# One edge tile in each eight chunks loaded row by row by SP in a two-layer graph network on Trainium2

## The chip, the core and the metric

The kernel runs on one core of a Trainium2 chip. Five engines work on their own instruction streams and meet through semaphores: TensorE (PE, matrix products and the loading of their stationary operand, PEld), VectorE (DVE), ScalarE (ACT), GpSimd (POOL) and SyncE (SP). SP does no arithmetic here: it only issues DMA transfers. ACT and POOL issue some as well. The metric is the device time of one execution in microseconds (us). The kernel before took 4951.64 us, the median of 7 runs (4927.57 to 4959.24).

## The reference

There are 12500 nodes with 256 features each and 200000 directed edges, given as `src` and `dst` and sorted by `dst`. Layer 0 normalises, applies a graph convolution twice between two dense products, and adds the input back. Layer 1 normalises, computes four attention heads and adds the input back. Cut to what matters:

```python
def _gcn_conv(h, W, b, src, dst, n):            # src, dst with a loop at each node added
    h = h @ W
    norm = dinv[src] * dinv[dst]                # dinv = 1/sqrt(number of edges into a node)
    return segment_sum(h[src] * norm[:, None], dst, n) + b

h = relu(layernorm(x))                          # layer 0
h = h @ W_pre + b_pre
h = relu(_gcn_conv(h, W1, b1, src, dst, n))
h = relu(_gcn_conv(h, W2, b2, src, dst, n))
x = x + h @ W_post + b_post
h = relu(layernorm(x))                          # layer 1
xt = (h @ weight).reshape(n, heads, out_ch)
alpha = softmax(leaky_relu(l(xt)[src] + r(xt)[dst], 0.01), axis=1)
x = x + broadcast(einsum('nh,nhd->nd', alpha[:n], xt[dst[:n]]))
```

The heavy part is `segment_sum(h[src])`: for each of the 200000 edges a row of 256 numbers is fetched by its node number, and the rows with the same destination are added up. It is done twice.

## The kernel before

**Stages.** A preparation of about 125 us counts the edges, normalises the nodes and writes the scaled rows to a table in device memory (`table1`, rows of 260 numbers: 256 features, a sum of scales, padding). The first convolution reads `table1` (its gathers run from 125 to 2353 us of the profiled span) and writes `table2` (rows of 256). The second reads `table2` (2395 to 4706 us) and also does everything per node that follows: the dense product, the residual, the second normalisation and the attention tables. A short mixing stage ends the kernel.

**Tiles.** The edges are cut into 112 chunks of 1792, each of 14 tiles (`J`) of 128 edges; the last chunk is shorter, so that a convolution has 1563 tiles. In `convolve` the loop over tiles does the following for tile `t`:

- POOL gathers the 128 rows that the tile's node numbers name into a slice of `fgot`, one row to a partition (L1128). `fgot` holds one chunk and has four buffers, so POOL can be at most four chunks ahead of PE.
- DVE makes, once per chunk, 0/1 matrices `fhot` that say which destination each edge belongs to (L1056).
- PE multiplies `fhot` and the rows into the accumulator `facc` (L1133, two instructions per tile), which adds up the rows by destination.

**Chunk ends and windows.** Destinations are worked through in 98 windows of 128 nodes. When a chunk is complete, ACT copies the accumulator to `fsums` (L1063). Steps that come later are entered in a list with a due tile and are carried out in the instruction streams when the loop has come to it (`at` and `run`). Eight tiles after the end of the chunk PE turns `fsums`, and with it the rows `self` of the next window, by transposing (L1019). Thirteen tiles after it DVE adds the turned sums to `buf` at an offset that it reads from memory into a register (L1075, L1079). `buf` holds the sums of two windows and a half, feature by feature. If a window is now complete, `shift` starts its finishing steps, takes a new `buf`, copies to it the part that stays (L1095) and the turned `self` rows (L1099), and calls `ready` for the window after.

**What SP does.** `ready` issues the loads of the next window. In the first convolution these are `fins` (L1152) and `self` (L1013). In the second they are `rb` (L1185), `fxb` (L1189) and `self`. `fins` and `rb` have four buffers and `fxb` three. The finishing steps of the second convolution also let SP store the new rows, `kept_x` (L1223), after DVE has written `fx` (L1221). SP carries these out strictly in the order of the program. The stores to `table2` and to the attention tables are issued by ACT.

**Finishing a window.** In the first convolution: a product with the weights, `fpo` (L1162, L1163), and a relu and a store by ACT. In the second: two products `fpz` and `fpo` (L1200, L1216), the residual `fx`, the normalisation, a turn `fpt` (L1242) and the attention products `fpx` (L1255), spread over 28 tiles.

The functions that the diff touches follow.

Of the kernel before, what the change touches and what calls it, by code (L numbers as in the profile page):

```python
# [8 lines left out]
F32 = mybir.dt.float32  # L9
BF16 = mybir.dt.bfloat16  # L10
I32 = mybir.dt.int32
# [6 lines left out]
P = 128  # L18
# [395 lines left out]
def fast_path(  # L414
# [26 lines left out]
    nc = tc.nc  # L441
    N, D = x.shape
    (E,) = src.shape
    H, C = attn_l.shape
    KC = D // P
    J = 14
    CE = J * P
    NCH = -(-E // CE)
# [5 lines left out]
    BW = OFF + P  # L454
# [11 lines left out]
    const = ctx.enter_context(tc.tile_pool(name="fconst", bufs=1))  # L466
# [25 lines left out]
    src_t = const.tile([P, NCH, J], I32, name="fsrc_t")  # L492
# [14 lines left out]

    bb = const.tile([2, D], F32, name="bb")

    with tc.tile_pool(name="fprep", bufs=1) as prep:  # L510


# [28 lines left out]
        def load_edges(e, pad, name):  # L541
            t = rows_p.tile([NCH, CE], I32, name=name)

            if last < CE:
                nc.vector.memset(t[:, last:], pad)

            some = (NCH - 1) // 16 * 16
            for c0, c1 in ((0, some), (some, NCH - 1)):
                nc.sync.dma_start(t[c0:c1, :],
                                  e[c0 * CE:c1 * CE].rearrange("(c e) -> c e", e=CE))  # L550
            nc.sync.dma_start(t[NCH - 1:NCH, :last], e[None, (NCH - 1) * CE:])
            return t
# [14 lines left out]
        def load_x(g, pool):  # L567
            n0, n1 = g * G * P, min((g + 1) * G * P, N)

            xt = pool.tile([P, G, D1], F32, name="fxt", bufs=XB if g < XB else NG - XB)  # L570
            nc.gpsimd.memset(xt[:, :, D:], 0.0)
            k, r = divmod(n1 - n0, P)
            if k < G:
                nc.gpsimd.memset(xt[:, k:, :], 0.0)
            nc.sync.dma_start(xt[:, :k, :D],
                              x[n0:n0 + k * P, :].rearrange("(c p) d -> p c d", p=P))
            if r:
                nc.sync.dma_start(xt[:r, k, :D], x[n0 + k * P:n1, :])
            xs.append(xt)

        XB = 11
        for g in range(XB):
            load_x(g, prep)
            if g == 1:
                src_r = load_edges(src, 0, "fsrc_r")


        zeros = prep.tile([1, 512], BF16, name="zeros")
# [378 lines left out]
    def convolve(ep, table, stride, width, ahead, with_sum, psum, prepare, finish):  # L967
# [28 lines left out]
        def run(now=None):  # L996

            while due:
                d = min(due, key=lambda d: (d["t"], d["n"]))
                if now is not None and d["t"] > now:  # L1000
                    return
                do(d)

        def new_buf():
            buf = work.tile([P, KC, BW], F32, name="buf", bufs=4)
            sbuf = work.tile([1, BW], F32, name="sbuf", bufs=4) if with_sum else None
            return buf, sbuf

# [14 lines left out]
        def new_turned(v):  # L1023
            v["pt"] = psum.tile([P, 2 * KC, P], F32, name="fturn", bufs=1)
            if with_sum:
                v["ps"] = psum.tile([1, 2, P], F32, name="fsum", bufs=1)

        state["buf"] = new_buf()
        for n0 in range(0, BW, P):
            v, n = {}, min(P, BW - n0)  # L1030
# [21 lines left out]
        def hot_of(c):  # L1052

            n = nj[c]
            h = ep.tile([P, J, P], F32, name="fhot", bufs=3)
            nc.vector.tensor_tensor(h[:, :n, :], iota_p[:, None, :].to_broadcast([P, n, P]),  # L1056
                                    to_t[:, c, :n, None].to_broadcast([P, n, P]), ALU.is_equal)
            return h

        def close(c, acc, t):  # L1060
# [24 lines left out]
            def shift(now):  # L1085
                w = state["w"]
                if w == complete[c + 1]:
                    return

                buf, sbuf = state["buf"]  # L1090
                pre, rows = state["next"]
                steps = finish(w, buf, sbuf, pre, state.get("bias"))
                if w + 1 < NT:
                    nxt, nxs = new_buf()
                    nc.vector.tensor_copy(nxt[:, :, :BW - P], buf[:, :, P:])  # L1095
                    if rows is None:
                        nc.vector.memset(nxt[:, :, BW - P:], 0.0)
                    else:
                        nc.vector.tensor_copy(nxt[:, :, BW - P:], v["pt"][:, KC:, :])  # L1099
                    if with_sum:  # L1100
                        nc.vector.tensor_copy(nxs[:, :BW - P], sbuf[:, P:])
                        if rows is None:
                            nc.vector.memset(nxs[:, BW - P:], 0.0)
                        else:
                            nc.vector.tensor_copy(nxs[:, BW - P:], v["ps"][:, 1, :])
                    state["buf"] = nxt, nxs

                then = None
                for i, (o, step, fills) in reversed(list(enumerate(steps))):
                    then = at(now + (i + 1 if near else o), lambda _, step=step: step(), fills, then)  # L1110
                state["w"] += 1
                ready(w + 1)
                if state["w"] < complete[c + 1]:
                    shift(now)
# [2 lines left out]
            at(t + (2 if c + 1 == NCH else 6 if near else 13), add)  # L1117

        tiles = [(c, j) for c in range(NCH) for j in range(nj[c])]
        hots = {0: hot_of(0)}  # L1120
        for t, (c, j) in enumerate(tiles):
            if j == 0:
                acc = psum.tile([P, width], F32, name="facc", bufs=2 if not with_sum else 3)

            if j == 0:
                gots = ep.tile([P, J, stride], F32, name="fgot", bufs=ahead)
            got = gots[:, j, :]
            nc.gpsimd.indirect_dma_start(  # L1128
                out=got, out_offset=None, in_=table[:],
                in_offset=bass.IndirectOffsetOnAxis(ap=src_t[:, c, j:j + 1], axis=0))  # L1130
            if j == 2 and c + 1 < NCH:
                hots[c + 1] = hot_of(c + 1)
            nc.tensor.matmul(acc, hots[c][:, j, :], got[:, :width], start=(j == 0),  # L1133
                             stop=(j == nj[c] - 1))
            if j == nj[c] - 1:
                close(c, acc, t)
            run(t)
# [37 lines left out]
    with tc.tile_pool(name="psum1", bufs=1, space=PSUM) as psum, \  # L1175
            tc.tile_pool(name="edges1", bufs=1) as ep, \
            tc.tile_pool(name="fwork1", bufs=2) as work:
        convolve(ep, table1, D1, D + 1, 4, True, psum, lambda w: prepare1(work, w),
                 lambda w, b, s, pre, _: finish1(work, psum, w, b, s, pre))
# [123 lines left out]
    ap = ctx.enter_context(tc.tile_pool(name="fatt", bufs=2))  # L1303
# [15 lines left out]
    with tc.tile_pool(name="psum2", bufs=1, space=PSUM) as psum, \  # L1319
            tc.tile_pool(name="edges2", bufs=1) as ep, \  # L1320
            tc.tile_pool(name="fwork2", bufs=2) as work:
        for c in range(EARLY):
            turn_hots(ap, c, load_ends(work, c, 1), EARLY)
        none = work.tile([P, LW, H], F32, name="none", bufs=1)
        nc.vector.memset(none, 0.0)
        nc.sync.dma_start(table_e[(NT - LW) * P:, :].rearrange("(w p) h -> p w h", p=P), none)

        from_all = work.tile([P, CE], I32, name="to_all", bufs=1)
        nc.sync.dma_start(from_all, src[:CE].partition_broadcast(P))
        for i in range(LW):  # L1330
            nc.vector.tensor_scalar(hot_l[i], from_all, float((NT - LW + i) * P), lane,
                                    op0=ALU.subtract, op1=ALU.is_equal)
        convolve(ep, table2, D, D, 4, False, psum, lambda w: prepare2(work, w),
                 lambda w, b, s, pre, bias: finish2(work, psum, w, b, pre, bias))

        for c in range(1, AC):
            own_rows(c)
# [111 lines left out]
def kernel(tc, *args):  # L1449
    nc = tc.nc  # L1450
    with tc.tile_pool(name="flag", bufs=1) as flag:
        bad = flag.tile([1, 1], I32, name="bad")
        with ExitStack() as ctx:
            with tc.manual_schedule():
                fast_path(ctx, tc, bad, *args)
        n_bad = nc.values_load(bad[0:1, 0:1], min_val=0, max_val=1 << 20,
                               skip_runtime_bounds_check_because="a count of chunks")
        with tc.If(n_bad > 0):
            with ExitStack() as ctx:
                general_path(ctx, tc, *args)  # L1460
# [27 lines left out]
```

## Time and profile before

| what | value |
|---|---|
| median of 7 runs | 4951.64 us (4927.57 to 4959.24) |
| the profiled execution's own time | 4976.77 us |
| its span, first to last instruction | 4975.0 us |
| mean granted TensorE clock | 0.709 |
| PE busy | 2659.2 us (53%) |
| POOL busy | 3116.0 us (63%) |
| DVE busy | 1206.1 us (24%) |
| ACT busy | 415.1 us (8%) |
| first convolution: first to last gather | 125 to 2353 us |
| second convolution: first to last gather | 2395 to 4706 us |
| mean load of the 16 DMA engines in the convolutions | 39% and 41% |

The profiled execution is 25 us longer than the median of the runs; its span and its own time differ by 1.8 us. Busy time counts work on data; instructions for registers, semaphores and the issuing of DMA transfers are not counted, so SP has no busy time at all and is read from the timeline and the waits. In a group of instructions the columns are line, engine, operation, output and inputs, number, then busy time and mean ns of one, then the idle time of the engine just before them and what ended most of it. "remote" as a releaser is a semaphore event whose origin the profile does not give; "issue" is time in which the engine waited for nothing that the profile shows. In a timeline the columns are start, duration, engine, line, operation, operands, the number of instructions put together, and the idle time before. A wait line names the waiting queue, whom it waited for, and the total, number and longest of the waits.

### The profile page before, as it was taken

The numbers are of one execution on the slowest core, as the hardware profiler recorded it, in microseconds if no ns is written. First come the engines' busy times: TensorE is split into PE (matmuls) and PEld (weight loads), VectorE is DVE, ScalarE is ACT, GpSimd is POOL, SyncE is SP. The second block draws the span as 40 slices with busy tenths as digits, with TensorE's granted clock in tenths as the row PEclk, the third lists the DMA queues.
The fourth block names the chain that finished last, engine by engine and source line by source line (L and its number), as shares of the span: only waits on it lengthen the run. The fifth ranks groups of instructions, "written<-read, shape, count | busy, mean of one in ns | idle before, by whom it ended". The sixth has DMA issues, their size and how long they took to land. (4 is left out here: it accounts for less than half of the span.)

```text
span 4975.0 us, 31762 instructions
## 1 busy us (share of the span) xinstructions
PE 2659.2 (53%) x10363; PEld 2032.3 (41%) x10363; DVE 1206.1 (24%) x2541; ACT 415.1 (8%) x1084; POOL 3116.0 (63%) x3346
## 2 busy tenths in 40 slices
PE   5355655555555655555454555555555455555553
PEld 4244433333444433333343444444444344444441
DVE  7121111111212111112221222222222222222236
ACT  5000000000000000000000100010011000000011
POOL 3666666666666666666566566666665566666533
PEclk6666666666666766666677777777777777777776
DMA  7433333333333333333334333444343344444335
GB/s 228 113 103 104 105 106 105 105 107 102 105 106 104 105 106 106 103 107 97 112 105 110 103 106 108 114 112 113 102 113 104 99 113 108 110 111 108 102 100 159
DMA packets 325909, 551.10 MB, mean 111 GB/s; under 512 B 96009, under 2 KB 224232, under 8 KB 325736
## 3 DMA queue, kind: packets, MB, share of 16 engines
q0 software_dynamic: 153520, 414.27, 31.2%
q1 hardware_dynamic: 126678, 118.54, 7.9%
q10 hardware_dynamic: 45538, 16.17, 1.3%
q8 instruction: 86, 1.41, 0.1%
q14 instruction: 87, 0.71, 0.1%
HBM read 495.47 MB, written 53.19 MB: 110 GB/s over the span
## 5 line engine op out<-in xcount | busy, mean ns | idle before, releaser
L1128 POOL DMA_INDIRECT fgot<-ftable,fsrc_t x3126 | 2974.1, 951 | 1616.6 <-issue 916.9
L1133 PE MATMUL facc<-fgot,fhot 128*128 128x257 f32 (+1 forms) x6252 | 1842.1, 437 | 553.3 <-issue 521.8
L1133 PEld LDWEIGHTS facc<-fgot,fhot 128*128 128x128 f32 x6252 | 1337.1, 222 | 897.1 <-issue 685.7
L1079 DVE TENSOR_TENSOR buf<-buf,fturn 128x256 f32 x224 | 94.5, 422 | 2059.4 <-remote 1633.8
L1056 DVE TENSOR_TENSOR fhot<-iota_p,to_t 128x1792 f32<-128x1792 f32 x224 | 448.3, 2003 | 0.1
L1242 PE MATMUL fpt<-fident,h 128*128 128x128 f32 x194 | 59.9, 407 | 607.9 <-ACT h L1237 538.8
L1162 PE MATMUL fpo<-wf,buf 128*128 128x256 f32 x388 | 149.6, 525 | 394.8 <-DVE buf L1079 298.5
L1242 PEld LDWEIGHTS fpt<-fident,h 128*128 128x128 f32 x194 | 27.1, 188 | 647.9 <-ACT h L1237 571.2
L1162 PEld LDWEIGHTS fpo<-wf,buf 128*128 128x128 f32 x388 | 96.2, 261 | 454.4 <-issue 339.3
L1216 PE MATMUL fpo<-fwo,fz 128*128 128x256 f32 x388 | 126.1, 454 | 255.3 <-issue 94.0
L1207 DVE SCALAR_TENSOR_TENSOR fy<-rb,fb2c,fpz 128x128 f32<-128x128 f32 x194 | 58.7, 344 | 737.5 <-remote 412.0
L1063 ACT ACTIVATE fsums<-facc 128x257 f32<-128x257 f32 (+1 forms) x224 | 85.8, 383 | 1808.4 <-remote 1361.4
L1221 DVE SCALAR_TENSOR_TENSOR fx<-fpo,fdinv,fxb 128x256 f32<-128x256 f32 x97 | 46.9, 483 | 737.2 <-remote 512.5
L1216 PEld LDWEIGHTS fpo<-fwo,fz 128*128 128x128 f32 x388 | 77.0, 218 | 269.9 <-ACT fz L1210 127.7
L1019 PE MATMUL fturn<-fident,fsums 128*128 128x128 f32 x448 | 105.4, 324 | 91.9 <-ACT fsums L1063 71.6
L1255 PE MATMUL fpx<-fwg,ht 128*128 128x4 f32 (+1 forms) x388 | 62.0, 267 | 171.8 <-ACT ht L1246 115.6
L1200 PE MATMUL fpz<-buf,fwb 128*128 128x128 f32 x776 | 152.7, 363 | 0.0
L1200 PEld LDWEIGHTS fpz<-buf,fwb 128*128 128x128 f32 x776 | 145.6, 277 | 1.1 <-DVE fy L1207 0.2
L1255 PEld LDWEIGHTS fpx<-fwg,ht 128*128 128x128 f32 x388 | 64.2, 210 | 185.2 <-ACT ht L1246 120.1
L1019 PEld LDWEIGHTS fturn<-fident,fsums 128*128 128x128 f32 x448 | 76.5, 174 | 140.4 <-ACT fsums L1063 81.3
L1397 POOL DMA_INDIRECT fal<-table_l,fsrc_t x84 | 80.4, 958 | 72.5 <-DVE fs L1404 47.8
L1387 PE MATMUL fends<-rows,hot_t 128*128 128x260 f32 x168 | 68.7, 553 | 96.1 <-issue 60.5
(212 smaller groups left out, 1644.5 us busy)
## 6 DMA issues: line engine op xcount, KB each, us to landing
fgot<-ftable,fsrc_t POOLq DMA_INDIRECT x3126
ftable<-fxt SPq DMA_DIRECT2D x14, 910.0 KB
self<-ftable SPq DMA_DIRECT2D x97, 130.0 KB
ftable<-fo ACTq DMA_DIRECT2D x98, 128.0 KB
kept_x<-fx SPq DMA_DIRECT2D x98, 128.0 KB
self<-ftable SPq DMA_DIRECT2D x97, 128.0 KB
fxb<-in_x_dram SPq DMA_DIRECT2D x97, 128.0 KB
fxt<-in_x_dram SPq DMA_DIRECT2D x13, 896.0 KB
```

Of the source, the lines that this page charges most:

```text
L1019: nc.tensor.transpose(v["pt"][:, i * KC + k, :], rows[:, k * P:(k + 1) * P], ident)
L1056: nc.vector.tensor_tensor(h[:, :n, :], iota_p[:, None, :].to_broadcast([P, n, P]), to_t[:, c, :n, None].to_broadcast([P, n, P]), ALU.is_equal)
L1063: nc.scalar.activation(sb, acc, AF.Copy)
L1079: nc.vector.tensor_add(b, b, v["pt"][:, :KC, :])
L1128: nc.gpsimd.indirect_dma_start(out=got, out_offset=None, in_=table[:], in_offset=bass.IndirectOffsetOnAxis(ap=src_t[:, c, j:j + 1], axis=0))
L1133: nc.tensor.matmul(acc, hots[c][:, j, :], got[:, :width], start=(j == 0), stop=(j == nj[c] - 1))
L1162: nc.tensor.matmul(po, buf[:, k, :P], wf[:, k, :], start=(k == 0), stop=False)
L1200: nc.tensor.matmul(pz[:, m, :], wb[:, k, m * P:(m + 1) * P], buf[:, k, :P], start=(k == 0), stop=(k == KC - 1))
L1216: nc.tensor.matmul(po, v["z"][:, m, :], wo[:, m, :], start=(m == 0), stop=(m == KC - 1))
L1242: nc.tensor.transpose(pt[:, k, :], v["h"][:, k * P:(k + 1) * P], ident)
L1255: nc.tensor.matmul(px, v["ht"][:, k, :], wg[:, k, d0:], start=(k == 0), stop=(k == KC - 1))
L1397: nc.gpsimd.indirect_dma_start(out=al[:, i, :], out_offset=None, in_=(table_l if c else table_e)[:], in_offset=bass.IndirectOffsetOnAxis(a ...
```

## The change

Every eighth chunk, beginning with chunk 3 (3, 11, ..., 99), has its last tile handled in another way: 13 tiles in each convolution. POOL does not gather them. SP reads the tile's 128 node numbers from a small table kept on the chip, `hand_i3`, 32 at a time into registers, and issues one DMA for each row, from the table's row of that number to one partition of a tile `hand3`. So a tile takes four bursts of 32 rows. The bursts are put into SP's stream at fixed places: the first about 132 tiles before the tile is used, the others 28 tiles apart, the last about 48 tiles before. For the first of these tiles there is not so much room, and its four bursts stand at tiles 0, 8, 17 and 26; the first burst of the next follows at 35. PE multiplies from `hand3` in place of `fgot`; the order of PE's, DVE's and ACT's work stays.

`hand3` has two buffers. The table of node numbers, 13 x 128, is loaded once in the preparation by one more DMA on SP. `buf` has three buffers in place of four. In line numbers, the changed kernel's `convolve` is moved down: its gather is at L1163, its matmul at L1168, its `self` load at L1023, its register load at L1145 and its row loads at L1149.

```diff
--- before.py
+++ after.py
@@ -507,6 +507,13 @@
 
     bb = const.tile([2, D], F32, name="bb")
 
+
+    HC = 8
+    HR = 32
+    NH = (E // CE - 1) // HC
+    HANDS = [(eng, of, const.tile([NH, P], I32, name=f"hand_i{of}"))
+             for eng, of in ((nc.sync, 3),)]
+
     with tc.tile_pool(name="fprep", bufs=1) as prep:
 
 
@@ -583,6 +590,9 @@
             load_x(g, prep)
             if g == 1:
                 src_r = load_edges(src, 0, "fsrc_r")
+                for _, of, idx in HANDS:
+                    nc.sync.dma_start(idx, src[:NH * HC * CE].rearrange(
+                        "(i c e) -> i c e", c=HC, e=CE)[:, of, CE - P:])
 
 
         zeros = prep.tile([1, 512], BF16, name="zeros")
@@ -1002,7 +1012,7 @@
                 do(d)
 
         def new_buf():
-            buf = work.tile([P, KC, BW], F32, name="buf", bufs=4)
+            buf = work.tile([P, KC, BW], F32, name="buf", bufs=3)
             sbuf = work.tile([1, BW], F32, name="sbuf", bufs=4) if with_sum else None
             return buf, sbuf
 
@@ -1117,6 +1127,27 @@
             at(t + (2 if c + 1 == NCH else 6 if near else 13), add)
 
         tiles = [(c, j) for c in range(NCH) for j in range(nj[c])]
+
+        hands = {}
+        rows_due = [[] for _ in range(NCH * J)]
+        for eng, of, idx in HANDS:
+            for i in range(NH):
+                due_by = (i * HC + of + 1) * J - 1
+                t0, t1 = max(due_by - HC * J - 20, 0), due_by - 20
+                for e0 in range(0, P, HR):
+                    rows_due[t0 + e0 * (t1 - t0) // P].append((eng, of, idx, i, e0))
+
+        def by_hand(t):
+            for eng, of, idx, i, e0 in rows_due[t]:
+                c = i * HC + of
+                if e0 == 0:
+                    hands[c, J - 1] = ep.tile([P, stride], F32, name=f"hand{of}", bufs=2)
+                _, nodes = nc.values_load_multi_w_load_instructions(
+                    idx[i:i + 1, e0:e0 + HR], engines=(eng.engine,), min_val=0, max_val=N - 1,
+                    skip_runtime_bounds_check_because="a node")
+                for k, n in enumerate(nodes):
+                    eng.dma_start(hands[c, J - 1][e0 + k:e0 + k + 1, :], table[bass.ds(n, 1), :])
+
         hots = {0: hot_of(0)}
         for t, (c, j) in enumerate(tiles):
             if j == 0:
@@ -1124,10 +1155,14 @@
 
             if j == 0:
                 gots = ep.tile([P, J, stride], F32, name="fgot", bufs=ahead)
-            got = gots[:, j, :]
-            nc.gpsimd.indirect_dma_start(
-                out=got, out_offset=None, in_=table[:],
-                in_offset=bass.IndirectOffsetOnAxis(ap=src_t[:, c, j:j + 1], axis=0))
+            by_hand(t)
+            if (c, j) in hands:
+                got = hands.pop((c, j))
+            else:
+                got = gots[:, j, :]
+                nc.gpsimd.indirect_dma_start(
+                    out=got, out_offset=None, in_=table[:],
+                    in_offset=bass.IndirectOffsetOnAxis(ap=src_t[:, c, j:j + 1], axis=0))
             if j == 2 and c + 1 < NCH:
                 hots[c + 1] = hot_of(c + 1)
             nc.tensor.matmul(acc, hots[c][:, j, :], got[:, :width], start=(j == 0),
```

## The prediction

> **What bounds the kernel now.** I read the page's busy times first, then the groups by line, then the timeline of POOL, of PE and of SP in a stretch of a convolution, then SP's waits.
>
> Busy times and costliest groups, from the page:
>
> ```profile
> span 4975.0 us, 31762 instructions
> ...
> PE 2659.2 (53%) x10363; PEld 2032.3 (41%) x10363; DVE 1206.1 (24%) x2541; ACT 415.1 (8%) x1084; POOL 3116.0 (63%) x3346
> ...
> L1128 POOL DMA_INDIRECT fgot<-ftable,fsrc_t x3126 | 2974.1, 951 | 1616.6 <-issue 916.9
> L1133 PE MATMUL facc<-fgot,fhot 128*128 128x257 f32 (+1 forms) x6252 | 1842.1, 437 | 553.3 <-issue 521.8
> ```
>
> No engine is full; POOL is busiest, and 95% of that is the gather of L1128. Its true rate is in the timeline of POOL alone, 1500 to 1530 us, in the first convolution:
>
> ```profile
> 1516.30 0.94 POOL L1128 DMA_INDIRECT fgot<-ftable,fsrc_t  x1 [0.30 <-issue]
> 1517.55 0.95 POOL L1128 DMA_INDIRECT fgot<-ftable,fsrc_t  x1 [0.30 <-issue]
> 1518.80 0.95 POOL L1128 DMA_INDIRECT fgot<-ftable,fsrc_t  x1 [0.30 <-issue]
> 1525.06 0.95 POOL L1128 DMA_INDIRECT fgot<-ftable,fsrc_t  x1 [5.31 <-remote]
> 1526.31 0.94 POOL L1128 DMA_INDIRECT fgot<-ftable,fsrc_t  x1 [0.30 <-issue]
> ```
>
> A gather starts each 1.2526 us, and then POOL stands still for 5.3 us: all four `fgot` buffers are full and PE has not given one back. This repeats each two chunks: 28 x 1.2526 + 5.1 = 40.2 us. In the second convolution the stop is mostly 2 to 3.5 us after each 14 gathers. PE over the same stretch:
>
> ```profile
> 1501.21 1.90 PE L1133 MATMUL facc<-fgot,fhot 128*128 128x257 f32 x8
> ...
> 1514.49 0.59 PE L1133 MATMUL facc<-fgot,fhot 128*128 128x257 f32 x1 [1.51 <-issue]
> 1517.29 0.59 PE L1133 MATMUL facc<-fgot,fhot 128*128 128x257 f32 x1 [2.21 <-issue]
> 1520.09 0.59 PE L1133 MATMUL facc<-fgot,fhot 128*128 128x257 f32 x1 [2.21 <-issue]
> ...
> 1528.10 1.57 PE L1133 MATMUL facc<-fgot,fhot 128*128 128x257 f32 x6
> ```
>
> PE does a burst (two matmuls of a tile in about 0.45 us), then creeps at 2.8 us a tile although the rows are there, and bursts again some us after POOL has stopped. I do not know why it creeps; it goes with POOL issuing. So the two are locked: POOL's gathers and its stop make the period, and one gather fewer should take its 1.25 us out of it.
>
> SP in the second convolution, 3001 to 3043 us (`kept_x` and the three loads of the next window):
>
> ```profile
> 3001.25 0.32 SPq L1223 DMA_DIRECT2D kept_x<-fx  x1
> 3001.62 0.43 SPq L1185 DMA_DIRECT2D rb<-roots  x1
> 3002.10 0.45 SPq L1189 DMA_DIRECT2D fxb<-in_x_dram  x1
> 3002.65 0.38 SPq L1013 DMA_DIRECT2D self<-ftable  x1
> 3021.39 0.32 SPq L1223 DMA_DIRECT2D kept_x<-fx  x1
> ```
>
> and SP's waits over the whole span:
>
> ```profile
> SPq L1223 <- DVE fx L1221: 1304.2, 55, 44.6
> SPq L1152 <- remote: 968.7, 36, 51.0
> SPq L1152 <- PE fpo L1163: 894.7, 48, 98.3
> ```
>
> SP is nearly always waiting. In the first convolution it waits for a free `fins` buffer and so stands three to four windows ahead. In the second it waits for the window's `fx`, works 1.8 us, and is idle for 18.4 us (3003.0 to 3021.4). That idle time is the cover of everything this change gives it.
>
> **The change, part by part.**
>
> *Gathers removed.* 13 per convolution, 26 of 3126. At 1.2526 us: 26 x 1.2526 = 32.6 us, if POOL's gathers set the period throughout. In the second convolution some stops last 8 to 10.7 us and end on PE's `facc`; there a shorter POOL stretch only waits longer. I take nine tenths: 29 us. Ends: 0 (PE sets the period) and 39 us (26 tiles at the second convolution's 1.50 us).
>
> *Rows added.* 26 tiles x 128 = 3328 row loads in 104 bursts on SP: a load of 32 registers, then for each row an address calculation and a DMA. The trace has no DMA with an address from a register and no such load. Nearest rows: SP's DMAs take 0.50 us (`fins`, one row), 0.53 (`self`, first convolution), 0.43 and 0.45 (`rb`, `fxb`), 0.32 (`kept_x`), with 0.05 us between; the address calculation is DVE's FUSED_REGOPS before L1079, 0.07 us; a load of one register is 0.30 us on DVE, 0.77 in SP's only case. Low end for a burst: 32 x (0.32 + 0.05) + 0.3 = 12 us, the calculation hidden. High end: 32 x (0.53 + 0.07 + 0.10) + 32 x 0.30 = 32 us, every register at the price of a load of one. I take 32 x (0.46 + 0.07 + 0.10) = 20 us and 3 us for the registers (between 0.8 and 9.6, nearer to the load that SP has made): 23 us. Over both convolutions 104 x 23 = 2.4 ms of SP's time, of which its 3.2 ms of waits are the cover.
>
> The Trainium skill ("Runtime: NRT & Kernel Launch", section "Instruction fetch mechanics") says a register load costs about 200 ns per register even in bulk; one register at 0.30 us in this trace neither confirms nor denies the bulk price. By that rule the 32 registers would be 6.4 us, the burst 26 us, and the result some 50 us worse than mine.
>
> *What stands behind a burst on SP.* One burst comes each 28 tiles. In the first convolution SP's lead takes it up, but at its start five bursts stand in a row ahead of window 1's `fins` and `self`: 134 + 5 x 23 = 249 us, and PE needs that `self` with tile 63, at 261 us. The second convolution starts likewise: 2416 + 5 x 23 = 2531, needed at 2537. Both just fit at 23 us; at 25 us they are 1 to 12 us late, at 30 us about 52 us together. In the second convolution's steady part, some bursts stand right behind `kept_x` and ahead of `rb`, `fxb` and `self`. There `self`, issued at 3042.9 and landing 2.5 us later, is used by PE's turn (L1019) at 3054.8, so only 9.5 us of the burst are hidden. I laid the new order of SP's stream over the issue times of before, with bursts of one length B, and added how late `self` lands for its turn: B = 18 us: 12 late, 42 us in all; 20: 14, 63; 23: 25, 112; 25: 26, 178; 30: 39, 540. PE's turn blocks the tiles behind it, and those hold POOL's buffers. But a PE that stops while creeping loses 2.8 us for a tile that a burst repairs in 0.45; bursts are about 15 of 40 us. So I let a half reach the end: 56 us at B = 23. Ends: 0 (all repaired) and 112.
>
> *PE's wait for a hand tile.* The rows come over eight DMA lanes, so the matmul has two more semaphore instructions (0.02 us, 52 in all: 1 us). The last burst is placed 48 tiles ahead of the use, some 67 us: hidden unless SP is behind by more than 40 us.
>
> *DMA queues and ACT.* 3328 rows of 1 KB are 3.4 MB beside 551; the DMA engines are at 33 to 40%. ACT's stores share the lanes with the rows: a store may wait for a row's landing, 2 to 5 us, and what it waits for (`fo`, three buffers) has a window's slack. Nothing. If completions of DMAs are what makes PE creep, 3328 more beside 3126 gathers could make it creep longer: unknown, bounded by nothing lost and by one slow tile (2.8 us) for each burst, 104 x 2.8 = 290 us.
>
> The skill's page "DMA: Bandwidth & Descriptors" ("Issuing engines are not separate DMA queues") says that issuing from another engine saves only the issuer's time. That speaks for counting POOL's 1.25 us and no transfer time. The sum is the same by it.
>
> *One more index load in the preparation* (13 x 128 numbers, one SP DMA, 0.5 us, beside `load_x`): under 1 us. *Three `buf` instead of four*: a new `buf` waits for the readers of the one three windows back; those are its own finish, 6 tiles after the shift, while windows are 16 tiles apart. Nothing; if it did wait, DVE's L1095 would show it.
>
> **Sum.** -29 + 56 + 1 + 1 = +29 us, against the profiled 4976.8 us: about 5006. That execution lies 25 us above the median of the runs shown (4951.6), so by the median the forecast is 4980 us, +0.6%. About 0.3% (15 us) is what a measurement of this kernel tells from no change.
>
> **The rivals.**
>
> 1. *Cover holds (faster).* Late `self` loads cost little because PE's backlog of landed tiles repairs them, or B is 18 us or less. Then -29 + 0 to 15: 4923 to 4938 us. For it: PE is 37 tiles behind POOL and has half its time free. Against it: POOL stops for want of buffers in each cycle, so PE has no slack to give. It turns where the stalls that reach the end equal 29 us: B about 20 us with a half, 0.63 us a row all told.
> 2. *No net change.* B is near 20 us, or PE sets the period so that nothing is gained and bursts fit: within 15 us of 4952. The long stops on `facc` speak for it; the first convolution's fixed 40.2 us against it.
> 3. *Long register loads.* B of 28 to 32 us: starts 35 to 70 us late, 300 to 600 us of late loads of which a half counts, less 29: 5080 to 5250 us. Only the one-register price speaks for it. Above 39 us a burst (28 tiles x 1.41 us) SP would set the pace, hundreds of us more; my high end does not reach it.
> 4. *The rows lengthen PE's creeping.* A quarter of the 290 us, less 29: about 4995 us, without any late `self`.
>
> **How the numbers follow.** Forecast (B 21 to 26, 4966 to 5050): 0.32. Rival 1: 0.36 over all its ways, but as a case with one size it is two (a short burst 0.18, a repaired delay 0.18), each less likely than the forecast. Rival 2: 0.14. Rival 3: 0.12. Rival 4: 0.06. Faster 0.36; same 0.14; slower 0.32 + 0.12 + 0.06 = 0.50. The range: down to the full gain with no loss, 4952 - 33 = 4919, taken to 4915; up to the lower part of rival 3, 5110, which leaves out its worse half and little else. The forecast's own range is 4966 to 5050.
>
> **What the profile after would show.** Gathers 3100 in number at the same 1.25 us; SP's bursts by their length (row to row under 0.63 us: rival 1; a register load over 6 us: rival 3); PE's waits on `self` at L1019 up from 21.8 us to about 110 if I am right, unchanged if rival 1 holds; POOL's stops the same length but the chunk pairs with a hand tile 1.25 us shorter; the first 300 us of each convolution without a gap if five bursts fit. I am wrong if SP's time per row is far from 0.63 us, or if PE's late turns vanish in its backlog.

## The result and the profile after

The changed kernel takes 5959 us (median of 19 runs, 5916 to 5997), the kernel before beside it 4954 us (46 runs, 4915 to 4993): a ratio of 1.2035, 95% interval 1.2013 to 1.2058. It is 1005 us slower. One number needs a word ahead of the experiments: the kernel before itself has two speeds, which change between groups of runs and not within one; beside the experiments it took 4958 to 4977 us in four groups and 4234 to 4243 in three, two chips showed both, and each experiment is compared with the kernel before of its own group. Where it takes about 4960 us, PE creeps as the prediction describes; where it takes about 4240 us, nothing creeps. The result was measured where it creeps. (`buf` holds three and a half windows of sums, 448 columns, and not two and a half as the description above has it.)

The busy times and the costliest groups of the changed kernel's page, with the columns as before:

```profile
span 5959.8 us, 41808 instructions
...
PE 2571.3 (43%) x10363; PEld 2022.1 (34%) x10363; DVE 1201.0 (20%) x2541; ACT 415.4 (7%) x1084; POOL 3099.0 (52%) x3320
...
L1163 POOL DMA_INDIRECT fgot<-ftable,fsrc_t x3100 | 2957.2, 954 | 2631.4 <-PE facc L1168 1408.0
L1168 PE MATMUL facc<-fgot,fhot 128*128 128x257 f32 (+1 forms) x6200 | 1784.1, 440 | 236.8 <-issue 228.3
...
L1029 PE MATMUL fturn<-fident,self 128*128 128x128 f32 x396 | 109.9, 372 | 2024.2 <-DMA self<-ftable 1982.1
```

The work costs what it did: a gather 954 ns (951 before), a matmul 440 (437). What is new is idle time. PE stands 1982 us in front of the turn of `self` (21.8 us before), and POOL's idle time has grown from 1617 to 2631 us, more than half of it now ended by PE giving a buffer back. SP, in the same profile, 1521 to 1578 us:

```profile
1529.49 43.66 SPq L1149 DMA_DIRECT2D hand<-ftable  x32
1573.25 0.53 SPq L1187 DMA_DIRECT2D fins<-root_t  x1
1573.83 0.58 SPq L1023 DMA_DIRECT2D self<-ftable  x1
1574.51 0.51 SPq L1187 DMA_DIRECT2D fins<-root_t  x1
1575.07 0.57 SPq L1023 DMA_DIRECT2D self<-ftable  x1
1577.95 1.96 SPq L1149 DMA_DIRECT2D hand<-ftable  x5
```

One burst of 32 rows takes 43.7 us, and two windows' loads wait behind it: SP has fallen behind and gives two `self` together. PE and POOL at the same place:

```profile
1576.24 0.69 PE L1029 MATMUL fturn<-fident,self 128*128 128x128 f32 x2 [35.28 <-DMA self<-ftable]
```

```profile
1522.22 0.94 POOL L1163 DMA_INDIRECT fgot<-ftable,fsrc_t  x1 [4.97 <-remote]
1581.32 0.95 POOL L1163 DMA_INDIRECT fgot<-ftable,fsrc_t  x1 [23.96 <-PE facc L1168]
```

PE waits 35.3 us for the `self` issued at 1573.8, and POOL's stop is 24 us where it was 5. SP's own waits, which were its cover:

```profile
SPq L1258 <- DVE fx L1256: 420.3, 45, 31.6
...
SPq L1187 <- PE fpo L1198: 75.5, 5, 23.6
SPq L1187 <- remote: 71.1, 3, 28.6
```

The waits on `fins` have fallen from 1863 to 147 us, and those on `fx` from 1304 to 420. The 104 bursts, each from its register load to its last row, add up to 4509 us: 46.8 us each in the first convolution, 39.9 in the second. From one hand tile's first burst to the next tile's the median is 202 and 200 us; in the first convolution four bursts of 46.8 are 187 us of that and the seven windows' loads take most of the rest: there SP is the bound. In the second, four bursts are 160 us of the 200, and in the rest SP still waits some 30 us for `fx`, which comes late because PE is late.

How late PE is against the profile of before, tile by tile, shows where the 1005 us came from: 93 us by tile 90, 526 us at the end of the first convolution, 90 us more in the first 112 tiles of the second, 993 us at its end. So the two starts cost 183 us, and the steady part some 40 us for each 112 tiles in the first convolution and some 35 in the second.

Why a burst is long is in the durations of the row instructions (minimum, median, maximum in ns), in this profile:

```profile
L1149 SPq FUSED_REGOPS  x3328: 1/37/1407, 135.9 to 5473.8; - x196
L1149 SPq MOVE hand<-ftable x3328: 1/29/1400, 136.0 to 5473.9; - x196
L1149 SPq DMA_DIRECT2D hand<-ftable x3328: 1/228/1398, 136.0 to 5473.9; - x196
```

and in a profile of the same kernel where nothing creeps (experiment after_again):

```profile
L1149 SPq FUSED_REGOPS  x3328: 37/37/47, 132.6 to 3811.7; - x196
L1149 SPq MOVE hand<-ftable x3328: 29/29/43, 132.6 to 3811.8; - x196
L1149 SPq DMA_DIRECT2D hand<-ftable x3328: 224/228/322, 132.7 to 3811.9; - x196
```

A row is three instructions, 0.41 us from row to row when SP is undisturbed. In the result's profile their records lie in steps of about 0.70 us for long stretches, whatever the instruction: a register operation there lasts 0.70 us, now and then 1.40, instead of 0.04. The length of a single record says little there: 719 of the 3328 DMA instructions are recorded with 20 ns or less, and undisturbed none takes under 224. So the steps are what is read here. Of the steps from row to row, 1587 are under 0.5 us, and 1237 are over 1.2 us and make up 3359 us of the bursts. Sorted by the number of gathers that POOL began in the 12 us before a row, the median step is 0.41 to 0.49 us with none to seven of them, 0.72 with eight, 2.11 with nine and 2.81 with ten. SP creeps like PE, while POOL's gathers follow one another. But the gathers alone do not do it: in after_again nine or ten of them stand in the 12 us before nearly every row, and the median step is 0.41 us.

### The profile page after: what moved, and what is told of

Its sections match the earlier page's. It is cut to its first block, busy times and chain, and to the rows that moved or that the text cites. A ratio compares the mean times of both kernels' runs of the same rounds, so it can differ in the third digit from the quotient of the medians.

```text
span 5959.8 us, 41808 instructions
## 1 busy us (share of the span) xinstructions
PE 2571.3 (43%) x10363; PEld 2022.1 (34%) x10363; DVE 1201.0 (20%) x2541; ACT 415.4 (7%) x1084; POOL 3099.0 (52%) x3320
## 5 line engine op out<-in xcount | busy, mean ns | idle before, releaser
L1163 POOL DMA_INDIRECT fgot<-ftable,fsrc_t x3100 | 2957.2, 954 | 2631.4 <-PE facc L1168 1408.0
L1168 PE MATMUL facc<-fgot,fhot 128*128 128x257 f32 (+1 forms) x6200 | 1784.1, 440 | 236.8 <-issue 228.3
L1168 PEld LDWEIGHTS facc<-fgot,fhot 128*128 128x128 f32 x6200 | 1357.8, 226 | 534.1 <-issue 309.0
L1029 PE MATMUL fturn<-fident,self 128*128 128x128 f32 x396 | 109.9, 372 | 2024.2 <-DMA self<-ftable 1982.1
L1029 PEld LDWEIGHTS fturn<-fident,self 128*128 128x128 f32 x396 | 55.0, 178 | 2060.7 <-DMA self<-ftable 1989.1
L1235 PE MATMUL fpz<-buf,fwb 128*128 128x128 f32 x776 | 137.0, 335 | 0.0
L1202 ACT ACTIVATE fo<-fpo,fdinv 128x256 f32<-128x256 f32 x97 | 46.0, 474 | 1241.7 <-remote 1087.1
L1235 PEld LDWEIGHTS fpz<-buf,fwb 128*128 128x128 f32 x776 | 129.8, 250 | 1.3 <-DVE fy L1242 0.2
L1197 PE MATMUL fpo<-wf,buf 128*128 128x256 f32 x388 | 102.7, 388 | 34.7 <-issue 24.5
L1298 ACT ACTIVATE fxa<-fpx 128x4 f32<-128x4 f32 (+1 forms) x95 | 18.4, 194 | 1299.1 <-PE fpx L1290 720.7
```

Of the source, the lines that this page charges most:

```text
L1029: nc.tensor.transpose(v["pt"][:, i * KC + k, :], rows[:, k * P:(k + 1) * P], ident)
L1163: nc.gpsimd.indirect_dma_start(out=got, out_offset=None, in_=table[:], in_offset=bass.IndirectOffsetOnAxis(ap=src_t[:, c, j:j + 1], axis=0))
L1197: nc.tensor.matmul(po, buf[:, k, :P], wf[:, k, :], start=(k == 0), stop=False)
L1235: nc.tensor.matmul(pz[:, m, :], wb[:, k, m * P:(m + 1) * P], buf[:, k, :P], start=(k == 0), stop=(k == KC - 1))
```

## The experiments

Theory A: SP's time for the rows is the loss; SP cannot finish four bursts and seven windows' loads in the time of 112 tiles, and PE waits for what stands behind the bursts. Theory B: the row transfers and their completions slow PE and POOL themselves. Theory C: the third `buf` is missed.

### The third buffer alone (bufs3)

```diff
-            buf = work.tile([P, KC, BW], F32, name="buf", bufs=4)
+            buf = work.tile([P, KC, BW], F32, name="buf", bufs=3)
```

> The kernel before with three buf instead of four, and nothing else. Theory A (SP is the bound: the row loads take SP longer than the tiles take PE, and the next window's self stands behind them) expects no difference, 4952 us within 15. Theory C (the third buffer of sums makes DVE wait) expects a good part of the 1005 us here.

Measured: 4242 us, the kernel before 4243; ratio 1.000 (0.999 to 1.0009). Theory C falls, for the condition in which this ran; no_rows_2 and fixed_2 below have three `buf` as well and lose nothing where PE creeps.

This run also showed that POOL can go without stops. Its gathers and matmuls:

```profile
L1128 POOL DMA_INDIRECT fgot<-ftable,fsrc_t x3126 | 2973.9, 951 | 975.9 <-issue 901.0
L1133 PE MATMUL facc<-fgot,fhot 128*128 128x257 f32 (+1 forms) x6252 | 2393.7, 501 | 946.9 <-DMA fgot<-ftable,fsrc_t 905.5
```

POOL's idle time is the 0.30 us behind each gather and little else (901 of 976 us), and PE waits for gathered rows. A gather costs the same 951 ns as in the profile of before.

### The gain alone (no_rows, no_rows_2)

```diff
-                    hands[c, J - 1] = ep.tile([P, stride], F32, name=f"hand{of}", bufs=2)
-                _, nodes = nc.values_load_multi_w_load_instructions(
...
-                    eng.dma_start(hands[c, J - 1][e0 + k:e0 + k + 1, :], table[bass.ds(n, 1), :])
+                    hands[c, J - 1] = blank
```

> The changed kernel with no row loads and no register loads: the 26 tiles are neither gathered nor loaded, PE multiplies a tile of zeros for them, so 3328 edges are missing from the sums. This is the gain by itself. If POOL's gathers and its stop set the period: 26 x 1.2526 = 33 us, 4920 us. If PE sets it: 4952 us.

> The kernel of no_rows again (the 26 tiles neither gathered nor loaded, 3328 edges missing), for a chip where PE and SP creep (before near 4960): the gain by itself there. 26 x 1.25 us if the cycle of gathers and stop keeps: 4927 us; 0 if PE sets the period: 4960. Where nothing creeps (before near 4240): 4209, as in no_rows.

Measured where nothing creeps: 4209.6 us against 4243.1, ratio 0.9928 (0.9912 to 0.9945): 33.5 us, close to 26 x 1.2526 = 32.6. Where PE creeps: 4964 against 4971, ratio 0.9974 (0.9952 to 0.9997): 7 us by the medians, 13 by the ratio, 24 at most. So the full gain is there only where POOL alone sets the time. Where PE and POOL are locked, most of a gather saved goes back into waiting: POOL's waits that ended with PE or with a remote event are 670 us in no_rows_2 and 623 in the profile of before.

### Rows loaded and gathers kept (rows_too)

```diff
-            if (c, j) in hands:
-                got = hands.pop((c, j))
-            else:
+            if True:
                 got = gots[:, j, :]
```

> The changed kernel with all 3126 gathers kept on POOL: the rows are loaded by SP as well and nobody reads them. Nothing waits for a hand tile. Theory A expects the same loss as the changed kernel, 5960 to 6000 us, with PE's wait for self near 1980 us. If the matmul's wait for hand tiles were the loss, 4952 us.

Measured: 4251 us against 4243, ratio 1.0018 (1.0007 to 1.0028). Nothing crept in this group, so it does not speak on the 1005 us. It shows that 3328 row loads on SP cost 8 us there, with bursts of 27.5 us (a bare burst is 15.2; the rest is rows waiting for stores of ACT in the DMA lanes: 811 us in 83 waits on the store of `fo` alone).

### One instruction for a row (fixed, fixed_2)

```diff
-                _, nodes = nc.values_load_multi_w_load_instructions(
-                    idx[i:i + 1, e0:e0 + HR], engines=(eng.engine,), min_val=0, max_val=N - 1,
-                    skip_runtime_bounds_check_because="a node")
-                for k, n in enumerate(nodes):
-                    eng.dma_start(hands[c, J - 1][e0 + k:e0 + k + 1, :], table[bass.ds(n, 1), :])
+                for k in range(HR):
+                    n = (1021 * i + 97 * (e0 + k)) % N
+                    eng.dma_start(hands[c, J - 1][e0 + k:e0 + k + 1, :], table[n:n + 1, :])
```

> The changed kernel with fixed row numbers in place of the edges' own: no register loads, and one instruction on SP for each row in place of three (the 26 tiles add up the wrong rows). Theory A with a slow pace per instruction of SP: a row falls from 1.37 us to some 0.6, a burst from 43 us to 18 to 25, SP is no longer the bound: 4950 to 5050 us. Theory B (each row DMA and its completions slow PE and POOL themselves, whoever issues it): 5900 to 5960 us, as the number of DMAs is the same.

> The kernel of fixed again (fixed row numbers, one SP instruction to a row, no register loads). Where PE and SP creep, theory A with a price of 0.70 us for each SP instruction: a row costs 0.70 to 0.9 us in place of 2.1 to 2.8 while POOL gathers, a burst 16 to 25 us, under the 34 at which SP becomes the bound: 4930 to 5010 us. If the price is for each DMA and not for each instruction: 5700 to 5960. Where nothing creeps: 4211, as in fixed.

Measured where nothing creeps: 4211 us, ratio 0.9931 (0.9914 to 0.9948), the same as leaving the rows out. Where PE and SP creep: 4972 against 4971 us, ratio 1.0005 (0.9983 to 1.0026). This is the run that decides between the theories. The 3328 row transfers, their completions, their lanes and the matmuls' waits for them are all there, and the loss is gone but for 7 us against no_rows_2 by the medians, 15 by the ratios, which is about their noise. Theory B falls. What was taken away is two of three instructions per row and the register loads: a burst is 28.2 us in place of 43.4, and PE's waits for `self` are back to small ones:

```profile
PE fturn L1029 <- DMA self<-ftable: 110.9, 26, 13.1
```

The price is one for each instruction: sorted as above, a row's median step here is 0.72 us with nine gathers and 1.38 with ten, 1.4 us less than with three instructions, which is twice 0.70. The burst is a little longer than the expected 16 to 25 us: 648 of its steps from row to row are still over 1.2 us. In part these are waits for ACT's stores in the DMA lanes, the semaphores that the rows share with them (217 us on the store of `fo`, 156 on that of `table_l`).

### The changed kernel again, and the windows' loads on ACT (after_again, on_act)

```diff
-            nc.sync.dma_start(s[:n, :], table[n0:n0 + n, :])
+            nc.scalar.dma_start(s[:n, :], table[n0:n0 + n, :])
```

and in the same way for `fins`, `rb`, `fxb` and `kept_x` (on_act; after_again has no edit).

> The changed kernel itself, beside the kernel before, because the kernel before took 4243 us where the first four experiments ran and 4954 us where the result was measured. If PE and SP again creep while POOL gathers (before at about 4950), theory A expects 5960 us again. If they don't (before at about 4243, POOL's gathers without stops), a row on SP is 0.41 us, POOL alone sets the time, and the change gives its 26 gathers: 4243 - 33 = 4210 us, at most 4225 with some late self loads.

> The changed kernel with the window's loads (fins, self, rb, fxb) and the store of kept_x issued by ACT, so that SP has the row loads alone and nothing stands behind them. Where PE and SP creep: theory A's first half (self behind the bursts) expects most of the loss gone; its second half (SP's capacity: 4 bursts of 43 us in 112 tiles are 172 us against 161 before) leaves the hand tiles themselves late, 5100 to 5400 us; theory B expects 5900. Where nothing creeps: as the changed kernel, 4205 to 4225 us.

Measured, where nothing creeps: 4210.9 us for the changed kernel, ratio 0.9945 (0.9929 to 0.9962), and 4208.1 for on_act, 0.9938 (0.9921 to 0.9954), against 4234. So the same kernel that is 20% slower in the result is 0.55% faster here, by 23 us. Its bursts are 27.2 us. SP in the first convolution:

```profile
1508.01 21.88 SPq L1149 DMA_DIRECT2D hand<-ftable  x32
1529.99 0.52 SPq L1187 DMA_DIRECT2D fins<-root_t  x1
1530.57 0.58 SPq L1023 DMA_DIRECT2D self<-ftable  x1
1531.24 0.52 SPq L1187 DMA_DIRECT2D fins<-root_t  x1
```

The order is the same as in the result's profile, with two windows behind a burst, and the burst half as long. PE waits 661 us for `self` here too (92 waits), and it costs little, because POOL sets the time and PE has time free.

### A longer burst, with the same transfers (pad8, pad16, pad16_act)

```diff
-                for k, n in enumerate(nodes):
+                for k in range(HR):
+                    if k % 4 == 0:                       # pad8; 2 in pad16 and pad16_act
+                        _, nodes = nc.values_load_multi_w_load_instructions(
...
-                    eng.dma_start(hands[c, J - 1][e0 + k:e0 + k + 1, :], table[bass.ds(n, 1), :])
+                    eng.dma_start(hands[c, J - 1][e0 + k:e0 + k + 1, :],
+                                  table[bass.ds(nodes[k], 1), :])
```

pad16_act has the edit of on_act as well.

> The changed kernel with the 32 numbers loaded anew after every 4 rows: 8 register loads of 2.07 us to a burst in place of one, so that SP is longer at a burst by 14.5 us and every transfer stays. Where nothing creeps the bare burst grows from 15.2 to 29.7 us, with waits for the DMA lanes some 36. Theory A (SP's time for four bursts and seven windows against the 139 us that POOL takes for 111 gathers): 4 x 36 + 8 = 152 us for each 112 tiles, 26 x 13 us more than 4211: about 4550 us (4250 to 4600). Theory B (the rows themselves disturb PE and POOL): no change, 4211.

> As pad8, with a new load after every 2 rows: 16 loads to a burst, 31 us more, a bare burst of 46 us, with lane waits 48: the length that it had where PE and SP crept (43 to 47). Theory A: 4 x 48 + 8 = 200 us for each 112 tiles, as in the result's trace (209): 26 x 61 us more than 4211, 5600 to 5900 us, with PE waiting on self. Theory B: 4211.

> pad16 with the windows' loads and stores issued by ACT, so that no self stands behind a burst. If the order on SP is the whole loss: 4210 to 4260 us. If SP's capacity is: hand tiles come late themselves, 4 x 48 = 192 us for each 112 tiles, 5400 to 5700 us, and PE waits at the matmul of the hand tile in place of the turn.

These ran where PE and SP creep (before 4976), and the numbers of theory A are for the other condition: bursts of 52.7, 64.9 and 78.6 us and 6908, 8170 and 8928 us, ratios of 1.393, 1.648 and 1.801. Theory B's "no change" fails in any case. The size can be checked by itself. From the changed kernel to pad8 the bursts grow by 9.3 us, 104 x 9.3 = 967 us of SP, and the time by 948. From pad8 to pad16 they grow by 12.2 us, 1269 us, and the time by 1262. Each us of SP is a us at the end (0.98 and 0.99). Followed back from the result in this proportion, the loss would be zero at 43.4 - 1005 / 104 = 33.7 us a burst; this is an estimate.

pad16_act tells the two halves of theory A apart. Nothing stands behind the bursts there, and it is slower still. What PE waits for has changed:

```profile
PE facc L1170 <- DMA hand<-ftable: 4648.9, 26, 195.4
```

All 26 hand tiles come late themselves. At this length of a burst it is SP's capacity, and the order on SP decides only which instruction of PE does the waiting. For the changed kernel's own bursts of 43.4 us this was not tried where PE creeps, as on_act ran in the other condition. In its first convolution bursts and loads fill SP's time; in the second, where SP still waits for `fx`, how the loss is shared between SP's capacity and the order on SP stays open.

### Half as many bursts (hc16)

```diff
-    HC = 8
+    HC = 16
```

> The changed kernel with one tile in sixteen chunks in place of eight (24 tiles less 12: 12 in all, 48 bursts). Where PE and SP creep: SP needs 2 x 47 + 14 us of each 161, it is no longer the bound, and what is left are late self loads behind single bursts: 4970 to 5150 us. If each burst costs its time whatever else SP has to do (48 x 10 us, half of the 1005): 5440. Where nothing creeps: 4243 - 15 = 4228.

Measured: 5204 us against 4971, ratio 1.046 (1.043 to 1.049), somewhat over the expected 4970 to 5150. The bursts are longer here, 55.3 us. PE's delay against the profile of before: 66 us by tile 90, then flat, 64 us at the end of the first convolution, in which 24 bursts stand. In the second: 82 us more in its first 112 tiles, then slowly up to 237 us, 91 us for the rest of the bursts. So once SP is not the bound, bursts are free in the first convolution, where SP is ahead by windows; about 20 of them cost 4.5 us each in the second, where it waits for each window's `fx`; and both starts cost nearly what they cost in the changed kernel (66 and 82 us against 93 and 90).

### Other distances of the gathers (paced_before to paced3_after)

```diff
                 in_offset=bass.IndirectOffsetOnAxis(ap=src_t[:, c, j:j + 1], axis=0))
+            nc.gpsimd.memset(idle, 0.0)    # idle: 128 x 28 in paced, 128 x 260 in paced2 and paced3
```

The kernels named "before" have it in the kernel before (paced2 and paced3 with three `buf`), those named "after" in the changed kernel.

> The kernel before with a small write by POOL (128 x 28 zeros, 0.115 us in the trace of before) after each gather of the convolutions, so that the gathers start about 1.4 us apart and not 1.25. If unbroken gathers at 1.25 us are what makes PE and SP creep, then on a chip where they creep: no creeping, POOL never stops for buffers, 3126 x 1.40 + 315 = 4690 to 4800 us. If creeping goes with POOL being busy at all: 4970 to 5400. Where nothing creeps: 4243 + 3126 x 0.15 = 4700.

> The changed kernel with the same small write after each gather. Where PE and SP creep, and the gathers' density is the cause: rows on SP at 0.4 to 0.6 us, bursts of 15 to 28 us, the loss gone: 4660 to 4800 us, 30 us under paced_before. If not: 5900 to 6300, with rows at 1.3 us or more. Where nothing creeps: 4670.

Measured, where PE and SP creep: 5004 us against 4977 (ratio 1.0055) and 6030 (1.211). This changed next to nothing in the distance: the small write took 0.14 us of the 0.30 us that lie between two gathers anyway, and the gathers still start 1.26 us apart. All went on creeping, bursts 43.9 us.

> The kernel before with three buf and a larger write by POOL after each gather (128 x 260 zeros, 0.315 us in the trace of before), because the small one fitted into the 0.30 us between two gathers and moved nothing (paced_before still has a gather each 1.26 us). Now the gathers should start 1.40 to 1.45 us apart. Where PE and SP creep: if it comes from gathers at 1.25 us, it is gone, POOL no longer stops and sets the time, 3126 x 1.43 + 315 = 4785 us (4690 to 4850); if it goes with POOL's being busy, the creeping stays and stops come on top: 5100 to 5600. Where nothing creeps: 4243 + 3126 x 0.18 = 4800.

> The changed kernel with the same larger write after each gather. Where PE and SP creep and the distance of the gathers is the cause: rows on SP at 0.4 to 0.6 us, bursts of 15 to 28 us, no loss, 4650 to 4820 us. If not: 6000 to 6600 with rows at 1.3 us or more. Where nothing creeps: 4765.

Measured, where nothing creeps: 4874 us and 4837 against 4234. The larger write makes a gather each 1.447 us; POOL sets the time and the change gives 37 us, 26 x 1.447. This is only the price of the pause.

> The kernel of paced2_before again (the kernel before with three buf and a gather each 1.45 us), because paced2 ran where nothing creeps and PE and SP did not show what they do at that distance where they creep. If they creep here (before near 4960): 4870 us as in paced2 if the distance of the gathers decides; 5050 to 5600 if not. If nothing creeps: 4873.

> The kernel of paced2_after again. If PE and SP creep here: 4837 us as in paced2 if the distance of the gathers decides; 5900 to 6600, with rows at 1.3 us or more, if not. If nothing creeps: 4837.

Measured, where the kernel before takes 4958 us: 4930 us, ratio 0.9943 (0.992 to 0.9966), and 4899 us, ratio 0.9883 (0.9847 to 0.9918). With 15% more distance the kernel before is not slower but faster, and the changed kernel has lost its loss: 4899 in place of 5959 to 6030. The gathers and matmuls of paced3_before:

```profile
L1129 POOL DMA_INDIRECT fgot<-ftable,fsrc_t x3126 | 3006.2, 962 | 546.8 <-issue 518.8 <-DMA ftable<-fo 13.8 <-DMA self<-ftable 9.7
...
L1135 PE MATMUL facc<-fgot,fhot 128*128 128x257 f32 (+1 forms) x6252 | 2785.8, 559 | 1120.2 <-DMA fgot<-ftable,fsrc_t 1079.2 <-issue 12.2 <-DVE fhot L1056 7.6
```

POOL has hardly any idle time beyond its issue gap, and PE waits for gathered rows, as where nothing creeps. In paced3_after the bursts are 32.6 us, and 476 of the steps from row to row are over 1.2 us (1237 in the result, 172 in paced2_after, where nothing creeps). So in this condition the creeping depends on how close the gathers follow each other: at 1.25 us it is there, at 1.45 us most of it is gone. The write by itself is not what removes it, as paced_before and paced_after have a write too and creep. paced3_after is the fastest of what was measured beside a kernel before of 4958 us. It is no better kernel in general: beside a kernel before of 4234 us the same program takes 4837.

## Why the prediction was wrong

**Gathers removed (29 us taken, 0 to 39).** In the result's condition the gain is 7 to 13 us (no_rows_2). The nine tenths were too many: the lock of POOL and PE does not pass a shorter POOL stretch on. Where nothing creeps it is the full 33.

**Rows added: the step that failed.** I put a burst at 23 us, with 32 as the high end; it is 43.4. The register load is 2.07 us (I took 3), and undisturbed a row is 0.41 us, less than my 0.63. But I took the price from SP's DMAs, which last 0.50 us in creeping stretches and out of them, when SP issues four of them and then waits. A burst is another matter: its 96 instructions run through whole creeping stretches, and there each takes about 0.70 us. I had described PE's creeping, had seen that it goes with POOL's gathers, and priced it as PE's own. The profile of before had a sign that it was not: SP's semaphore instructions of L1013 have a median of 17 ns and a maximum of 1223, those of L1223 17 and 723. I also read the creeping too small: 2.8 us is the step from one matmul to the next, and a tile has two, so that a tile takes 4 to 5 us in the stretch shown. The load of 32 registers takes 2.07 us in the median, 65 ns a register; the Trainium skill's 200 ns ("Runtime: NRT & Kernel Launch", section "Instruction fetch mechanics") would have made it 6.4 us, as an estimate. For these loads, from the table `hand_i3` on the chip, the measurement decides against it, and it was not the term that mattered.

**What stands behind a burst (56 us; none in the first convolution).** The place was right and the size was not. At 23 us the starts just fit; the first bursts took 92.9 and 86.2 us, because POOL's first 69 gathers follow one another without a stop, and the starts cost 183 us. PE also waited twice for a hand tile itself there, 93 us, where I had written "hidden unless SP is behind by more than 40 us". In the steady part I let SP's lead take up the first convolution; with 187 us of bursts in a cycle of 161 there is no lead, and it lost 40 us for each 112 tiles.

**The bound I named and left out.** Rival 3 says that above 39 us a burst SP would set the pace, hundreds of us more, and that my high end does not reach it. This is what happened, with the limit at 33.7 us by the estimate above. The rivals were complete but for the price of a row. (Rival 3's own sum, half of 300 to 600 us less 29, gives 5073 to 5223 us and not 5080 to 5250.)

**What was right.** Three `buf` cost nothing (bufs3, no_rows_2). Transfers and lanes cost nearly nothing: 7 us by the medians between fixed_2 and no_rows_2, so rival 4 falls. What the gathers and matmuls cost did not change. The order of events at a late `self` (turn, then POOL's buffers) is the one foretold. Late `self` loads alone are cheap while SP is not the bound: 4.5 us for each burst in hc16's second convolution.

## What to carry to other kernels

A queue that mostly waits has free time, but the price of work moved into it must be taken from stretches where the rest of the core does what it will be doing then; a slowness seen on one engine is to be looked for on the others, in the maximum beside the median. Count instructions, not transfers: where PE and SP creep, the same 3328 transfers cost next to nothing with one instruction each and a thousand us with three; where nothing creeps, both kernels take 4211 us. Work out at which length the queue becomes the bound, and where the estimate's upper end comes near it (32 of 39 us here), price that case as a likely one.

## What the runs showed of the hardware

- Register, move and DMA-issuing instructions of SP take 37, 29 and 228 ns undisturbed (after_again). In the result's profile they take about 0.70 us each, whatever they are, in stretches in which POOL has begun nine or ten gathers in 12 us. PE's matmuls come 1.4 to 2.8 us apart in such a stretch of the profile of before. The granted clock is 0.50 there, but a matmul then lasts 0.59 us in place of 0.38, so the clock does not account for the distance.
- A load of 32 registers takes 2.07 to 2.12 us on SP (the medians of after, after_again, pad8 and pad16). A load of one took 0.30 us on DVE.
- One program has two speeds, 4234 to 4243 and 4954 to 4977 us, with the same mean duration of a gather (951 ns) and the same most frequent duration of a matmul (0.38 us). It is no property of a chip: two chips showed both at different times. In the slower one the distance of the gathers decides how much creeps (1.25 us much, 1.45 us little). There the trace also holds far fewer completions of DMAs, 15249 in the profile of before against 67143 in that of bufs3, and instructions recorded as shorter than they ever are undisturbed. What differs between the two conditions was not found. One candidate was not tested: every execution of the experiments has a recorded span and clock, so no run tells whether the recording itself takes part in the creeping.
- A row on SP waits for ACT's stores in the DMA lanes: in after_again 798 us in 83 waits on the store of `fo` and 384 on those of the attention tables, together nearly all of what makes a bare burst of 15.2 us into one of 27.2.
